# A graph-attention and hypergraph kernel on one core: plain products for the first two pairs' features, another order in the prologue, and the last pair's sums of h on VectorE

## The chip, the cores and the metric

The kernel runs on one core of a Trainium2 chip. A core has TensorE (PE, with its weight loads shown as PEld), VectorE (DVE), ScalarE (ACT), GpSimd (POOL) and SyncE (SP), which here only issues transfers. The metric is the device time of one execution in microseconds (us). The kernel before took 2590.04 us, the median of three runs from 2588.01 to 2591.15.

## The reference

The input x has 128 graphs of 128 nodes with 512 features, adj the 128 x 128 matrix of each graph (0 or 1, with ones on the diagonal). All is float32. Two layers follow one another, each with a residual and a layer norm:

```
feats = x @ W (8 heads of 64)                       # features
dense = leaky(feats.a_self[i] + feats.a_neigh[j]) + BIG * (adj - 1)
att   = softmax(dense, over j);  y = relu(att @ feats + b0)
x1    = layernorm(x + y)

H = (adj != 0);  prop(v) = Dn * H @ (Be * H^T @ v)   # Dn, Be from sums of H and adj's first row
h  = relu(prop(x1 @ W1^T) + b1);  h = layernorm(h) * gamma + beta     # 1024 wide
out = layernorm(x1 + (prop(h @ W2^T) + b2) + x1)
```

## The kernel before, in words

**Tiling.** The graphs are worked off in 64 pairs. Everything of a pair sits in tiles of 128 partitions: its x and adj, the scores nb (2 graphs x 8 heads x 128), the attention's result y, the hidden layer h (1024 wide) and the output o. Weights stay in SBUF throughout. W, W1 and W2 are each cut into a 2 x 2 grid of blocks.

**Three block products.** The features (tile names pf), the hidden layer (ph) and the second product (py) are each computed with seven block products in place of eight. For this the operands need sums and differences of blocks: those of the weights are made once (`prepare_first_sums`, `prepare_hidden`, `prepare_output_block_sums`, all on DVE), those of the data once per pair (`x_sums` on POOL with tile xS, `z_sums` with zS, `h_sums` with hS, through the helper `first_sums`). `chain` puts the seven products in the order 1, 2, 6, 5, 7, 4, 3 as far as its list of times says so: 1, 6, 7 and 4 go on in the same PSUM bank X, from which ACT copies the states after 1, 6 and 7; 2 goes to Y; 5 and 3 to W. `f_sum`, `h_sum` and `y_sum` add the parts up.

**Stages of a pair.** `nodes` computes Dn from adj's first row, turns it with a DVE transpose into the tile dr, and `write_nodes` writes that to DRAM (dd_d), from where `spread_nodes` reads it back to all partitions. `edges` and `scale_edges` make H^T and its scaled copy, `propagator` multiplies the two (pd), `r_evict` gives R. `x_transpose` turns x, the feature product follows, `spread_rows` sends the attention's row terms through DRAM (rd), `neighbours` reads them back to all partitions (nb). POOL adds the mask (`masked`), ACT applies the leaky function and the exponential, DVE finds the maxima in between (`largest`, tile nm). The exponentials are transposed through DRAM (`e_write`, `e_read`, `e_transpose`: tiles ed, eb, eT), for pair 0 alone on PE (`e_transpose_first`, tile pet). `attend` (pav), `attended`, `add_bias` (POOL), `residual`, `rstds`, `first_shift` (sh) and `first_output` (ACT) give x1. `propagate` (pz), the ph chain, `relu`, `square`, `squares` (POOL), `h_sums` (POOL), the py chain, `h_rstd`, `y_scale` and `output` (pq) and the norm end with the store.

**What sets the order.** Each step is entered with a lag in pairs and a time; it is put at (pair + lag) x 38.6 + time. All steps of all pairs and the one-off steps of `todo` are sorted by this number and issued in that order, so each engine's queue is fixed by hand. The function `shift` changes the times of pairs 0 and 1. Each engine works its queue in order. Most work tiles have one buffer, some two (`bufs=2`), so a step also waits until the buffer's former content has been read.

**Transfers.** SP issues nearly all of them, in the same order; a transfer's issue also waits for the landing of the one eight places before it, since eight counters are shared by SP's and ACT's transfers. At the start, code outside the timed list issues them: pair 0's adj, half of w0, pair 0's blocks of x and adj, the other half of w0, pair 1's adj, then w2 (2 MB) and w1 (2 MB). ACT issues seven small loads (attention vectors, biases, gamma, beta).

**Weights' preparation.** `prepare_first` multiplies w0 by the attention vectors (DVE and POOL) and reduces, ACT copies w0 beside the result. `prepare_output` multiplies w2 with gamma and beta on PE (pv, L232), `prepare_output_sums` sends the two rows through DRAM (sums_d, gw, bw_bc), `prepare_output_blocks` scales w2 with them (16 DVE instructions, L254).

Of the kernel before, what the change touches and what calls it, by code (L numbers as in the profile page):

```python
# [20 lines left out]
def kernel(  # L21
# [41 lines left out]

    nc = tc.nc
    G, N, F = x.shape
    P = 128
# [20 lines left out]
        return psum.tile([P, HALF], F32, tag="bank", name=name)  # L89


    st = {}

    def load(p):
        s = st[p] = {}
        gs = slice(2 * p, 2 * p + 2)
        s["a"] = work.tile([P, 2, N], F32, tag="a", name=f"a_{p}", bufs=2)
        nc.sync.dma_start(s["a"], adj[gs].rearrange("g n e -> n g e"))
        s["w"] = work.tile([P, 2, N], F32, tag="w", name=f"w_{p}")
        for g in range(2):  # L100
            nc.sync.dma_start(s["w"][:, g, :], adj[2 * p + g, 0, :].partition_broadcast(P))

    def load_blocks(p):
        s = st[p]
        gs = slice(2 * p, 2 * p + 2)

        s["xb"] = work.tile([P, 2 * NB, P], F32, tag="xb", name=f"xb_{p}")
        rows = x[gs].rearrange("g (b n) (f c) -> f n (g b) c", b=NB, f=NB)
        for f in range(NB):
            nc.sync.dma_start(s["xb"][f * B:(f + 1) * B], rows[f])  # L110

    def load_edges(p):
        s = st[p]

        s["ab"] = work.tile([P, 2 * NB, B], F32, tag="ab", name=f"ab_{p}")
        rows = adj[2 * p:2 * p + 2].rearrange("g (b n) (f e) -> f n (g b) e", b=NB, f=NB)
        for f in range(NB):
            nc.sync.dma_start(s["ab"][f * B:(f + 1) * B], rows[f])

    load(0)  # L120


    def block(dst, ap, i, j, rows, cols):
# [11 lines left out]
    for dst, i, j in ((w0_sb[:, 0], 0, 0), (w0_sb[:, 1], 1, 0), (w0_12, 0, 1), (w0_sb[:, 2], 1, 1)):  # L135
        raw = work.tile([P, KF // 2, QU], F32, tag=("eT", "nb", "sq", "hS")[2 * i + j], name=f"w0_raw{i}{j}")
        nc.sync.dma_start(
            raw, w0.rearrange("(p k) c -> p k c", k=KF)
            [:, i * KF // 2:(i + 1) * KF // 2, j * QU:(j + 1) * QU],
        )  # L140
        if (i, j) == (1, 0):
            load_blocks(0)
            load_edges(0)
        w0_blocks.append((dst, raw.rearrange("p k (h u) -> p k h u", h=HH), j))

    def everywhere(ap, n, name):
# [3 lines left out]

    as_bc = everywhere(a_self, F, "as_bc")
    an_bc = everywhere(a_neigh, F, "an_bc")
    load(1)
    b0_bc = everywhere(b0, F, "b0_bc")
    b2_bc = everywhere(b2, F, "b2_bc")
    bw_bc = const.tile([P, F], F32, name="bw_bc")
# [3 lines left out]
    for t, ap in ((b1_sb, b1), (gb[:, 0, :], gamma), (gb[:, 1, :], beta)):  # L160
        nc.scalar.dma_start(t, ap.rearrange("(k p) -> p k", p=P))

    staged = work.tile([P, 2, DH], F32, tag="h", name="staged")

    w2_sb = const.tile([P, 7, KH // 2, QU + 1], F32, name="w2_sb")
    w2_12 = staged[:, 1, :].rearrange("p (k c) -> p k c", k=KH // 2)
    w2_blocks = ((w2_sb[:, 0, :, :QU], 0, 0), (w2_12, 0, 1), (w2_sb[:, 1, :, :QU], 1, 0),
                 (w2_sb[:, 2, :, :QU], 1, 1))
    for dst, i, j in w2_blocks:
        block(dst, w2t, i, j, DH // 2, QU)  # L170

    w1_sb = const.tile([P, 7, KF // 2, HALF], F32, name="w1_sb")
    w1_21 = staged[:, 0, :].rearrange("p (k c) -> p k c", k=KF // 2)
    for dst, i, j in ((w1_sb[:, 0], 0, 0), (w1_21, 0, 1), (w1_sb[:, 1], 1, 0), (w1_sb[:, 2], 1, 1)):
        block(dst, w1t, i, j, F // 2, HALF)

    ident = const.tile([P, P], F32, name="ident")
    make_identity(nc, ident)
# [8 lines left out]
    dn = const.tile([P, B], F32, name="dn")  # L187
    nc.gpsimd.memset(dn, 0.0)

    def second_sums(eng, w, b12):  # L190

        b11, b21, b22, t4, t1, t2, t3 = (w[i] for i in range(7))
        eng.tensor_tensor(t1, b12, b11, op=ALU.subtract)
        eng.tensor_tensor(t2, b22, t1, op=ALU.subtract)
        eng.tensor_tensor(t3, b22, b12, op=ALU.subtract)
        eng.tensor_tensor(t4, b21, t2, op=ALU.subtract)

    def prepare_first(half):
        for n, (dst, raw, j) in list(enumerate(w0_blocks))[2 * half:2 * half + 2]:
# [8 lines left out]
                nc.vector.tensor_reduce(dst[:, :, :, c], t, AX.X, ALU.add)  # L208

    def prepare_first_sums():  # L210
        second_sums(nc.vector, [w0_sb[:, i] for i in range(7)], w0_12)

    def prepare_hidden(i):
        a11, a12, a22, s1, s2, s3, s4 = (w1_sb[:, i] for i in range(7))
# [31 lines left out]
            nc.sync.dma_start(t, sums_d[c].partition_broadcast(P))  # L246
        made["gw"] = gw

    def prepare_output_blocks():
        gw = made["gw"]  # L250
        for blk, i, j in w2_blocks:
            for k in range(KH // 2):
                c = i * KH // 2 + k
                nc.vector.scalar_tensor_tensor(  # L254
                    blk[:, k, :], blk[:, k, :], gb[:, 0, c:c + 1], gw[:, j * QU:(j + 1) * QU],
                    op0=ALU.mult, op1=ALU.subtract,
                )

    def prepare_output_block_sums():
        second_sums(nc.vector, [w2_sb[:, i, :, :QU] for i in range(7)], w2_12)  # L260
        for i in (0, 1, 5):
            nc.gpsimd.memset(w2_sb[:, i, :, QU:], 1.0 / DH)


    steps = []

    def step(lag, time, skip_first=False):
        def keep(fn):
            steps.append((lag, time, fn, skip_first))
            return fn  # L270
        return keep

    def at(lag, time, fn, *args, skip_first=False):
        step(lag, time, skip_first)(lambda p, s: fn(p, s, *args))

    def chain(kind, lag, times, multiply, w, extra=0):

        tag = "chain" if w == HALF else "half"

        def product(p, s, i):
            where, start = {1: ("X", 1), 2: ("Y", 1), 6: ("X", 0), 5: ("W", 1), 7: ("X", 0),
                            4: ("X", 0), 3: ("W", 0)}[i]
            if start:
                s[kind, where] = bank(f"{kind}{where}_{p}")
            multiply(s, i, s[kind, where], start)

        def copy(p, s, i):
            n = w + (extra if i < 2 else 0)
            t = s[kind, i] = work.tile([P, HALF if w == HALF else FW], F32, tag=f"{tag}_{i}", name=f"{kind}{i}_{p}")
            nc.scalar.copy(t[:, :n], s[kind, "X"][:, :n])  # L294

        for i, t in zip((1, 2, 6, 5, 7, 4, 3), times):
            at(lag, t, product, i)
        for i, t in enumerate(times[7:]):
            at(lag, t, copy, i)

# [103 lines left out]
        first_sums(s, "xS", f"xS_{p}", halves(s["xT"], KF // 2), i, nc.gpsimd, "xS")  # L406

    for i in range(4):
        at(1, 6.1 + 0.7 * i, x_sums, i)

    def rows_product(s, i, a, sums, w, n, nk, extra, to, start):

# [12 lines left out]
    def feature(s, i, to, start):  # L425
# [1 line left out]
                     w0_sb.rearrange("p b k h u -> p b k (h u)"), FW, KF // 2, 0, to, start)  # L427

    chain("pf", 1, (16.2, 17.1, 18.0, 18.9, 19.8, 22.4, 23.3, 17.3, 19.0, 20.8),
          feature, FW)  # L430

    def by_head(t):
        return t[:, :FW].rearrange("p (h u) -> p h u", h=HH)
# [6 lines left out]
        else:  # L440
            nc.vector.tensor_tensor(dst, by_head(s["pf", i]), by_head(s["pf", where]), op=ALU.add)

    at(1, 18.2, f_sum, 0, 0, 0, "Y")
    at(1, 21.4, f_sum, 1, 1, 2, "W")
    at(1, 24.4, f_sum, 0, 1, 1, "W")
    at(1, 23.4, f_sum, 1, 0, None, "X")

    @step(1, 25.0)
    def spread_rows(p, s):
# [110 lines left out]
    for (g, q), tm, (lag, tl), (lagx, tx), te, tt in (  # L560
        ((0, 0), 31.0, (1, 33.2), (1, 33.9), 2.7, 18.1), ((0, 1), 32.2, (1, 35.0), (1, 36.7), 4.6, 18.15),
        ((1, 0), 34.2, (1, 37.5), (2, 2.0), 7.8, 21.5), ((1, 1), 35.4, (2, 6.0), (2, 7.3), 7.9, 21.55),
    ):
        at(1, tm, masked, g, q)
        at(lag, tl, leaky, g, q)
        at(lagx, tx, largest, g, q)
        at(2, te, exponential, g, q)
        at(2, tt, e_transpose, g, q, skip_first=True)

    for g in range(2):  # L570
        at(2, (6.2, 10.9)[g], e_write, g, skip_first=True)
        at(2, (10.0, 14.9)[g], e_read, g, skip_first=True)

# [185 lines left out]

    def h_sums(p, s, i):
        first_sums(s, "hS", f"hS_{p}", halves(s["h"], KH // 2), i,
                   nc.gpsimd, "hS")

    at(3, 20.9, h_sums, 0)
    at(3, 22.2, h_sums, 1)
# [82 lines left out]
    def o_norm(p, s):  # L850
# [4 lines left out]

    T = 38.6
    todo = [
        (11.1, prepare_first, (0,)), (12.0, prepare_first, (1,)), (13.0, prepare_first_sums, ()),
        (65.0, prepare_output, ()), (71.4, prepare_output_sums, ()), (73.7, prepare_hidden, (0,)),
        (75.6, prepare_hidden, (1,)), (77.5, prepare_hidden, (2,)), (77.6, prepare_hidden, (3,)),  # L860
        (82.0, prepare_output_blocks, ()), (83.0, prepare_output_block_sums, ()),
    ]

    def on_pair(fn, p):
        fn(p, st[p])

    def shift(p, lag, time):

        if p == 0:
            if lag == 0:  # L870
                return 2.5 if time < 12.0 else 0.0
            if lag == 1 and 4.0 < time < 10.0:
                return -T + (6.8 if time < 6.0 else 8.0)
            if lag == 2 and time < 8.5:
                return -0.8 * time
        if p == 1 and lag == 1:
            if time < 4.0:
                return -6.0
            return -17.5 if time < 10.0 else -13.0 if time < 12.0 else -23.1 if time < 26.0 else 0.0
        return 0.0  # L880

    for p in range(PAIRS):
        if p > 1:
            todo.append((p * T, load, (p,)))
        if p:
            todo.append((p * T + 19.0, load_blocks, (p,)))
            todo.append((p * T + 28.5, load_edges, (p,)))
        for lag, time, fn, skip in steps:
            if p or not skip:
                todo.append(((p + lag) * T + time + shift(p, lag, time), on_pair, (fn, p)))  # L890
    todo.append((2 * T + 2.1, on_pair, (e_transpose_first, 0)))

    with tc.manual_schedule():
        for _, fn, args in sorted(todo, key=lambda e: e[0]):
# [43 lines left out]
```

## Time and profile before

The profiled execution took 2588.97 us, its span in the trace 2587.2 us, so 1.8 us lie around the span.

| | busy in the span | share |
|---|---|---|
| PE | 2513.1 us | 97% |
| PEld | 2271.3 us | 88% |
| DVE | 2137.3 us | 83% |
| POOL | 1721.5 us | 67% |
| ACT | 1516.3 us | 59% |

In the middle of the run one pair follows the other every 38.6 us. The profile's views used below: the chain of work that ended last, followed back from the last instruction; the list of waits, by waiter and releaser; busy time by stage of the run; and the timeline of one engine, which gives the start of each instruction, its length, the engine, the line of the kernel, what it writes and reads, how many were merged, and in brackets how long the engine had been idle before it and what ended that.

### The profile page before, as it was taken

What the parts mean: (1) busy time and instruction counts of PE and PEld (TensorE: products, weight loads), DVE (VectorE), ACT (ScalarE), POOL (GpSimd) and SP (SyncE); (2) the same over time, 40 slices, a digit from 0 to 9 for tenths busy, and PEclk for the clock granted to TensorE, in tenths of its full rate; (3) what the DMA queues carried; (4) which work ended last, traced back from release to release, by engine and by line L of the source; (5) the groups of instructions that cost most, each with busy time, mean ns of one, the idle gap of its engine ahead of it and who ended that gap; (6) DMA issues with size and microseconds to landing.
All of it is one profiled execution on the core that took longest, in us unless ns stands there. A gap on an engine that the chain in (4) does not pass through costs nothing.

```text
span 2587.2 us, 48238 instructions
## 1 busy us (share of the span) xinstructions
PE 2513.1 (97%) x16304; PEld 2271.3 (88%) x16304; DVE 2137.3 (83%) x4648; ACT 1516.3 (59%) x4297; POOL 1721.5 (67%) x1809
## 2 busy tenths in 40 slices
PE   4799999999999999999999999999999999999997
PEld 2699899899899899899899889999999899999986
DVE  4788888888888888888888888888898888888874
ACT  1465565565565565565565565565565565565562
POOL 3467667667667667667667667667667667766663
PEclk8799999999999999999999999999999999999998
DMA  6344444444444444444444544444444444444430
GB/s 165 106 138 127 149 137 130 141 141 128 143 141 130 145 139 130 146 134 130 144 136 127 150 130 131 144 137 131 142 135 134 142 137 132 143 137 132 143 115 20
DMA packets 428250, 345.57 MB, mean 134 GB/s; under 512 B 146658, under 2 KB 377058, under 8 KB 428004
## 3 DMA queue, kind: packets, MB, share of 16 engines
q1 hardware_dynamic: 424308, 341.43, 43.8%
q8 instruction: 130, 2.13, 0.3%
q10 hardware_dynamic: 3696, 1.06, 0.2%
q14 instruction: 116, 0.95, 0.1%
HBM read 240.66 MB, written 101.72 MB: 132 GB/s over the span
## 4 chain that ended last, share of the span: by engine, by line
PE 91%; DMA 4%; DVE 2%; issue 1%; POOL 1%; ACT 0%; SPq 0%; ACTq 0%; POOLq 0%; DVEq 0%
PE phX L705 18%; PE pyX L418 15%; PE pfX L418 9%; PE phW L705 9%; PE pyW L418 8%; PE pav L579 8%; PE phY L705 4%; PE pz L670 4%; PE pfW L418 4%; PE pq L829 4%; PE pyY L418 4%; PE pfY L418 2%; DMA nb<-rd 2%; PE pd L374 1%; DMA rd<-rows 1%
## 5 line engine op out<-in xcount | busy, mean ns | idle before, releaser
L294 ACT COPY py<-pyX 128x257 f32<-128x257 f32 (+1 forms) x192 | 71.7, 374 | 552.7 <-PE pyX L418 552.7
L705 PEld LDWEIGHTS phX<-zS,w_sb 128*128 128x128 f32 x3072 | 363.0, 192 | 31.2 <-issue 31.2
L499 POOL TENSOR_TENSOR nb<-nb,neg 128x512 f32<-128x512 f32 x256 | 320.3, 1272 | 99.9 <-DMA nb<-rd 54.1
L705 PE MATMUL phX<-zS,w_sb 128*128 128x128 f32 x3072 | 374.2, 275 | 0.7 <-issue 0.7
L756 POOL TENSOR_TENSOR sq<-sq 128x512 f32<-128x512 f32 (+2 forms) x384 | 342.3, 891 | 29.6 <-ACT sq L745 8.6
L506 ACT ACTIVATE nb<-nb,ft 128x128 f32<-128x128 f32 x1024 | 325.4, 390 | 39.1 <-POOL nb L499 34.5
L520 ACT ACTIVATE nb<-nb,nm 128x128 f32<-128x128 f32 x1024 | 320.2, 393 | 1.0 <-DVE nm L512 1.0
L626 POOL TENSOR_TENSOR rso<-veo,mhalf 128x2 f32<-128x2 f32 x64 | 44.8, 700 | 344.9 <-DVE veo L624 329.3
L610 DVE SCALAR_TENSOR_TENSOR y<-y,x 128x512 f32<-128x512 f32 x128 | 154.6, 1208 | 133.2 <-POOL y L603 132.9
L579 PEld LDWEIGHTS pav<-ft,eT 128*128 128x128 f32 x2048 | 252.1, 194 | 11.3 <-DVE eT L541 3.4
L418 PE MATMUL pyX<-w_sb,hS 128*128 128x257 f32 (+1 forms) x1024 | 248.2, 384 | 5.0 <-POOL hS L400 5.0
L579 PE MATMUL pav<-ft,eT 128*128 128x65 f32 x2048 | 246.5, 274 | 3.2 <-DVE eT L541 3.2
L735 ACT ACTIVATE h<-h,b_sb 128x128 f32<-128x128 f32 x768 | 241.2, 392 | 11.6 <-DVE h L720 11.6
L418 PE MATMUL pyW<-w_sb,hS 128*128 128x256 f32 x1024 | 244.1, 380 | 3.5 <-DVE y L788 3.5
L418 PE MATMUL pyX<-w_sb,h 128*128 128x257 f32 (+1 forms) x1024 | 244.3, 381 | 0.0
L418 PEld LDWEIGHTS pyW<-w_sb,hS 128*128 128x128 f32 x1024 | 192.2, 189 | 37.0 <-DVE y L788 9.9
L603 POOL TENSOR_TENSOR y<-y,b_bc 128x512 f32<-128x512 f32 x128 | 162.1, 1266 | 89.4 <-DVE y L594 89.3
L418 PEld LDWEIGHTS pyX<-w_sb,hS 128*128 128x128 f32 x1024 | 190.2, 191 | 30.4 <-POOL hS L400 5.4
L418 PEld LDWEIGHTS pyX<-w_sb,h 128*128 128x128 f32 x1024 | 190.1, 191 | 25.2
L400 POOL TENSOR_TENSOR xS<-xT 128x256 f32<-128x256 f32 x128 | 121.4, 948 | 102.3 <-DVE xT L338 102.3
L512 DVE TENSOR_REDUCE nm<-nb 128x4 f32<-128x512 f32 x256 | 174.2, 680 | 3.8 <-ACT nb L506 1.9
L294 ACT COPY ph<-phX 128x512 f32<-128x512 f32 x192 | 112.4, 585 | 96.4 <-PE phX L705 93.3
(121 smaller groups left out, 5838.5 us busy)
## 6 DMA issues: line engine op xcount, KB each, us to landing
nb<-rd SPq DMA_DIRECT2D x128, 512.0 KB, 5.8
ed<-nb SPq DMA_DIRECT2D x126, 512.0 KB, 3.1
eb<-ed SPq DMA_DIRECT2D x504, 128.0 KB, 2.7
xb<-in_x_dram SPq DMA_DIRECT2D x256, 128.0 KB, 3.0
x<-in_x_dram SPq DMA_DIRECT2D x64, 512.0 KB, 7.1
out_dram<-o SPq DMA_DIRECT2D x64, 512.0 KB, 2.9
a<-in_adj_dram SPq DMA_DIRECT2D x64, 128.0 KB, 6.2
w<-in_adj_dram SPq DMA_DIRECT2D x128, 64.0 KB, 3.8
```

The source lines that it names most:

```text
L294: nc.scalar.copy(t[:, :n], s[kind, "X"][:, :n])
L418: nc.tensor.matmul(to[:, :n], lhs[:, k, :], rhs[:, k, :n], start=bool(start) and k == 0, stop=(k == nk - 1), skip_group_check=True,)
L499: nc.gpsimd.tensor_tensor(t, t, neg[:, :, None, :].to_broadcast([P, NB, HH, B]), op=ALU.add)
L506: nc.scalar.activation(t, t, AF.Prelu, bias=s["ft"][:, g, h, 0:1], alpha=SLOPE)
L512: nc.vector.tensor_reduce(s["nm"][:, g, hs], scores(p, s, g, hs).rearrange("p b h j -> p h b j"), AX.XY, ALU.max, negate=True,)
L520: nc.scalar.activation(t, t, AF.Exp, bias=s["nm"][:, g, h:h + 1])
L579: nc.tensor.matmul(t[:, h * (U + 1):(h + 1) * (U + 1)], s["eT"][:, g, q * HH + h, :], s["ft"][:, g, q * HH + h, 2:], start=True, stop=True,)
L603: nc.gpsimd.tensor_tensor(s["y"][:, g, :], s["y"][:, g, :], b0_bc, op=ALU.add)
L610: nc.vector.scalar_tensor_tensor(y, y, 0.0, s["x"][:, g, :], op0=ALU.max, op1=ALU.add)
L705: nc.tensor.matmul(to[:, m * N:(m + 1) * N], w[:, k, m * P:(m + 1) * P], rhs[:, k, :], start=bool(start) and m == 0 and k == 0, stop=(k == ...
L735: nc.scalar.activation(dst[:, k, :], src[:, k, :], AF.Relu, bias=b1_sb[:, c:c + 1])
L756: nc.gpsimd.tensor_tensor(t[:, :n, :], t[:, :n, :], t[:, n:2 * n, :], op=ALU.add)
```

## The change

It touches three places.

- **First two pairs' features.** Pairs 0 and 1 no longer use the seven-product chain, its sums xS and `f_sum` (`since=2`). `plain_features` does the eight block products directly from w0's four blocks, for each of the two graphs into two PSUM banks; `plain_features_out` moves the banks to the feature tile, two on ACT and two on DVE. w0's block differences are then first used by pair 2, and `prepare_first_sums` is placed later.
- **Prologue.** All of w0 is loaded first, then pair 0's adj; pair 0's blocks of x and adj are issued from ACT. Pair 1's loads, w2 and half of w1 become timed steps behind pair 0's row terms (nb), the other half of w1 comes after pair 1's. `shift` is replaced by a table of times for single steps of pairs 0 and 1. `prepare_output` (pv) now stands between pair 0's two attention products, and w1's and w2's preparation on DVE is placed behind pair 0's first layer, that of w2 in two parts. The tiles that take w1's and w2's odd block are separate ones instead of one.
- **Last pair.** For pair 63 `h_sums` runs on VectorE; its first attention products and what follows on them are placed later, behind the first py product of pair 62; of its own py chain, product 2 is placed ahead of product 6.

The core of the diff:

```diff
-    load(0)
...
-        if (i, j) == (1, 0):
-            load_blocks(0)
-            load_edges(0)
...
-    load(1)
+    load(0)
+    load_blocks(0, nc.scalar)
+    load_edges(0, nc.scalar)
...
-    for dst, i, j in w2_blocks:
-        block(dst, w2t, i, j, DH // 2, QU)
...
+    def load_weights(blocks, ap, rows, cols):
+        for dst, i, j in blocks:
+            block(dst, ap, i, j, rows, cols)
...
+    def plain_features(p, s):
+        s["pf"] = [[bank(f"pf_{p}_{g}{j}") for j in range(2)] for g in range(2)]
+        for i in range(2):
+            for j in range(2):
+                w = (w0_sb[:, 0], w0_12, w0_sb[:, 1], w0_sb[:, 2])[2 * i + j]
+                for g in range(2):
+                    for k in range(KF // 2):
+                        nc.tensor.matmul(
+                            s["pf"][g][j][:, :FW], s["xT"][:, g, i * KF // 2 + k, :],
+                            w[:, k].rearrange("p h u -> p (h u)"), start=(i == 0 and k == 0),
+                            stop=(i == 1 and k == KF // 2 - 1), skip_group_check=True,
+                        )
+
+    def plain_features_out(p, s):
+        s["ft"] = fts[p]
+        for j in range(2):
+            for g in range(2):
+                (nc.scalar.copy, nc.vector.tensor_copy)[g](
+                    s["ft"][:, g, j * HH:(j + 1) * HH, :UW], by_head(s["pf"][g][j])
+                )
...
-                   nc.gpsimd, "hS")
+                   nc.vector if p == PAIRS - 1 else nc.gpsimd, "hS")
...
-        (11.1, prepare_first, (0,)), (12.0, prepare_first, (1,)), (13.0, prepare_first_sums, ()),
-        (65.0, prepare_output, ()), (71.4, prepare_output_sums, ()), (73.7, prepare_hidden, (0,)),
-        (75.6, prepare_hidden, (1,)), (77.5, prepare_hidden, (2,)), (77.6, prepare_hidden, (3,)),
-        (82.0, prepare_output_blocks, ()), (83.0, prepare_output_block_sums, ()),
+        (11.1, prepare_first, (0,)), (12.0, prepare_first, (1,)), (77.9, prepare_first_sums, ()),
+        (11.8, load_blocks, (1,)), (15.65, load, (1,)), (15.7, load_edges, (1,)),
+        (15.8, load_weights, (w2_blocks, w2t, DH // 2, QU)),
+        (16.0, load_weights, (w1_blocks[:2], w1t, F // 2, HALF)),
+        (80.2, load_weights, (w1_blocks[2:], w1t, F // 2, HALF)),
+        (103.0, prepare_output, ()), (116.5, prepare_output_sums, ()),
+        (112.0, prepare_hidden, (0,)), (112.5, prepare_hidden, (1,)),
+        (114.5, prepare_hidden, (2,)), (115.0, prepare_hidden, (3,)),
+        (122.4, prepare_output_blocks, (slice(0, 2),)),
+        (128.4, prepare_output_blocks, (slice(2, 4),)),
+        (130.6, prepare_output_block_sums, (slice(0, 2),)),
+        (132.8, prepare_output_block_sums, (slice(2, 4),)),
+        (100.0, prepare_mean_columns, ()),
...
+    first = {
+        ("nodes", 0): 15.0, ("write_nodes", 0): 16.5, ("spread_nodes", 0): 18.5,
+        ("x_transpose", 0): 11.5, ("edges", 0): 15.2, ("scale_edges", 0): 15.4,
+        ("spread_rows", 0): 13.5, ("neighbours", 0): 14.0, ("load_rows", 0): 14.2,
+        ("propagator", 0): 103.5, ("r_evict", 0): 104.0,
+        ("nodes", 1): 17.6, ("write_nodes", 1): 17.9, ("x_transpose", 1): 14.5,
+        ("edges", 1): 110.4, ("scale_edges", 1): 110.5,
+        ("spread_rows", 1): 79.9, ("neighbours", 1): 80.0,
+        ("propagator", 1): 117.7, ("r_evict", 1): 118.0,
+    }
...
+        (0, plain_features, 12.5), (0, plain_features_out, 13.0), (0, e_transpose_first, 79.3),
+        (1, plain_features, 16.2), (1, plain_features_out, 79.2),
...
+            if p == PAIRS - 1:
...
+                time = {
+                    ("attend", 0): 24.25, ("attended", 0): 25.5, ("add_bias", 0): 25.6,
+                    ("h_sums", 0): 19.1, ("h_sums", 1): 19.2,
+                    ("product", 2): 25.0 if (lag, time) > (3, 20.0) else time,
+                }.get((name,) + args[:1], time)
```

## The prediction

> **What bounds the kernel now.** I read first the chain of work that ended last, then PE's waits in the long middle, then the engines' busy time by stage. The chain's first line:
>
> ```profile
> PE 91%; DMA 4%; DVE 2%; issue 1%; POOL 1%; ACT 0%; SPq 0%; ACTq 0%; POOLq 0%; DVEq 0%
> ```
>
> PE's waits between 134 and 2470 us (waiter, releaser, us in total, times, longest):
>
> ```profile
> PE pyW L418 <- DVE y L788: 3.0, 8, 1.0
> ```
>
> Busy time by stage (stretch, its length, busy us of PE, PEld, DVE, ACT, POOL with counts, then granted clock, DMA share, GB/s):
>
> ```profile
> 0.00:96.40 96.40, 44.67 (x161) 30.17 (x161) 55.86 (x123) 23.64 (x65) 28.42 (x39) 0.77 0.52 139
> 96.40:134.50 38.10, 37.38 (x251) 34.76 (x252) 26.73 (x63) 23.46 (x67) 25.56 (x27) 1.00 0.42 126
> 134.50:2464.40 2329.90, 2326.81 (x15243) 2114.21 (x15242) 1985.21 (x4321) 1415.98 (x4020) 1608.60 (x1680) 1.00 0.46 137
> 2464.40:2541.10 76.70, 73.03 (x478) 66.13 (x478) 54.00 (x112) 42.46 (x119) 44.10 (x46) 0.98 0.27 92
> 2541.10:2587.20 46.10, 31.24 (x178) 25.99 (x177) 15.50 (x33) 10.77 (x28) 14.83 (x17) 0.89 0.06 23
> ```
>
> The middle is PE's alone: it waits 3 us in 2330, and the change leaves the order of every engine there as it was. So only the first 114 us and the last 70 can move. The prologue, from the timelines (start, us, engine, line, what, count, idle before it and its releaser):
>
> ```profile
> 31.88 8.21 SPq L324 DMA_DIRECT2D dd_d<-dr  x2
> 39.51 0.21 DVE L319 STREAM_TRANSPOSE dr<-dn 128x32 f32<-128x32 f32 x1 [4.75 <-DMA dd_d<-dr]
> 43.20 0.23 DVE L453 STREAM_TRANSPOSE rows<-ft 128x32 f32<-128x32 f32 x1
> 51.73 4.92 POOL L499 TENSOR_TENSOR nb<-nb,neg 128x512 f32<-128x512 f32 x4 [1.79 <-DMA nb<-rd]
> 68.31 1.63 DVE L254 SCALAR_TENSOR_TENSOR w_sb<-w_sb,gb,gw 128x256 f32<-128x256 f32 x4
> 92.88 3.38 PE L670 MATMUL pz<-R,y 128*128 128x128 f32 x16 [14.50 <-ACT y L647]
> 114.40 1.90 PE L579 MATMUL pav<-ft,eT 128*128 128x65 f32 x16
> ```
>
> DVE waits 4.75 us for a 16 KB write behind the weights' loads; pair 0's rows leave at 43.4; DVE then prepares w2 from 68.3 to 79.3 before pair 0's attention, so pz waits until 92.88. From pz on PE runs through. The tail:
>
> ```profile
> 2516.23 1.95 PE L705 MATMUL phW<-zT,w_sb 128*128 128x128 f32 x16
> 2521.39 2.63 PE L579 MATMUL pav<-ft,eT 128*128 128x65 f32 x16 [3.21 <-DVE eT L541]
> 2523.82 3.03 PE L418 MATMUL pyX<-w_sb,h 128*128 128x257 f32 x8
> ...
> 2555.15 1.91 PE L418 MATMUL pyX<-w_sb,h 128*128 128x257 f32 x8
> 2562.01 3.80 PE L418 MATMUL pyX<-w_sb,hS 128*128 128x257 f32 x8 [4.96 <-POOL hS L400]
> 2565.60 2.57 PE L418 MATMUL pyY<-w_sb,h 128*128 128x257 f32 x8
> ```
>
> Two gaps, 3.21 and 4.96 us, each followed by matmuls at up to twice their time (3.80 for 1.73 in the middle).
>
> **The Trainium skill.** "TensorE: Matmul & The Clock Gate", Part 1, says PE's clock halves after an idle window of about 3.4 us and comes back after a busy one. The trace agrees on half (264-column matmuls 0.52 us each when cold, 0.222 warm), though pv, started cold, takes about 5.4 us to warm, and pav, 7.09 us on end, doesn't warm it. "SBUF — State Buffer", Who interferes with whom: a DVE instruction with two SBUF inputs and a GpSimd one block each other. Here a 128x528 difference takes 0.67 us alone and 1.04 to 1.22 beside POOL. "DMA: Bandwidth & Descriptors", Queues, rings and completion order: each ring is consumed in order. The write dd_d took 7.5 us behind three loads of w1, and 1.4 with nothing ahead.
>
> **Prologue, step by step.** (1) The w0 loads go first, so DVE and POOL can start at 4.7 rather than 8.3 us. But ACT now issues 15 loads (7 before) ahead of its copies of w0. At 0.45 us each and with the waits for earlier landings (4 to 6 us per load), its last, beta, goes out by about 15 (before, beta's issue alone held ACT 3.3 us). Table load 1.28, copy 0.62: first matmul at 17.0 (bounds 15.3 and 18). DVE's last reduction is done by then.
> (2) Pair 0's plain product has 16 matmuls, 32 passes, against 28, without the sums on POOL and copies between. 5.2 us cold (10 passes), 22 x 0.222: 27.1. Copy 0.42 and transpose 0.23: rows at 27.9, 15.5 us earlier. Pair 1's 32 passes (7.1 warm) follow while PE would wait for exponentials: free, as are POOL's three memsets of 0.17, put where POOL is idle.
> (3) Rows to POOL's mask takes 51.73 - 43.43 = 8.3: mask at 36.2.
> (4) Here the gain sticks. SP issues behind the rows' reads: x, a, w twice, ab four times, w2 four times, w1 twice, and only then pair 0's dd_d. Each waits for a landing some eight loads back. w2 starts at 39 (x landed), its 2 MB and 1 MB of w1 at 360 GB/s (350 to 375 between 21 and 25 us of this trace) take 8.5 from 40.5, and dd_d lands at 49.6. DVE's dr of pair 1 waits for it (one buffer), and behind dr on DVE stand pair 0's maxima, for which ACT's exponentials wait. Without it they would start at 41; they start at 49.9. Bounds 47 and 52.
> (5) Leaky and exponentials, 1.25 per group of four, five left: 56.8. Copies of pair 1's features 0.65, first eT 0.5, two pav cold 3.5, y and gbs 0.9: pv at 62.6. pv now stands between pair 0's two attentions; cold it costs 9.7 (45.94 to 55.67 before), warm 6.9. I take 9.7. The w0 sums fall beside idle POOL and hide. pav, pd, pav 2.2, y 0.6: 75.1. From the last y to pz, 92.88 - 85.79 = 7.1: **pz at 82.1**, 10.7 earlier.
> (6) The preparation that DVE did before pz comes after it. From the shift (sh, done 0.9 ahead of pz, 81.2) to pair 1's first eT, DVE has edges and their scaling 1.8, hidden 4 x 1.13, sums 0.7, 16 scalings of w2 6.3, its four differences 4.7 (18.0 added), and 11.6 as before (maxima 2.4, edges 1.4, transposes 2.1, skip 1.25, scale and nodes 1.7, R 0.3, h 1.8, eT 0.6). 29.6, plus 1 for POOL (0 to 3.5): eT at 111.9. PE is through pf at pz + 21.5 as before + 0.4 for pair 1's pd, at 104.0, and waits 8 us; resuming cold costs 2.4 (5 us at half speed). So pav stands as if begun at 114.3, against 114.4. **Prologue: 0.1 gained, in fact nothing**; bounds -6.6 (load bounds early, pv warm) and +4.8 (late, POOL in the way).
>
> **Tail.** (7) For pair 63, pav of group 0 goes behind py 1 of pair 62: 1.74 us of matmul fills the first gap, PE idles 1.6 and stays warm. py 6 starts at 2524.9 (hS on POOL ends 2524.8) instead of 2528.6. Yet pz then waits for the shifted output, 2536.4 as before, against PE's 2539.1: 2.6 gained, 1.2 if the clock drops anyway.
> (8) Pair 63's sums of h: POOL's three squares 2.7 and three sums 3.8 become DVE sums behind the norm of pair 62's output. On the shifted clock h is ready at 2554.7, DVE free 2555.2, two sums at 0.6 alone or 1.2 beside POOL's squares: 2556.6 to 2557.9. py 2 is pulled ahead of py 6 and fills 1.74. py 6, 7, 5, pm, 4, 3 from 2557.6: five at 1.73 to 1.79, 0.45 for the copy between 6 and 7 that py 2 used to hide, pm 0.15: 2566.9 against 2575.3. The last 11.9 us stay. **Tail: 8.4** (5.5 to 8.9).
>
> Sum: 8.5. The profiled execution took 2588.97 (span 2587.2 and 1.8 around it), 1.07 below the median 2590.04. It becomes 2580.5, the median 2581.
>
> **Rivals.** *Loads in time* (ends lower): dd_d lands when nodes are ready (41) or pv is warm and POOL out of the way. For: 3 MB need only start earlier than SP's waits allow in my count. Against: the 4.75 us wait above. DVE's 29.6 still stands between, so 5 to 9 us: 2572 to 2576. *Prologue eats the tail*: eT is 5 to 9 us later than in (6) because DVE's two-input steps run beside POOL's z and x sums, which take 5.8 us there. For: 0.67 against 1.22. It leaves 2586 to 2590, no change. *The write behind the weights decides* (slower): if dd_d lands after 63.3, 13.7 us past my count, each us comes out at the end and the kernel passes 2595. That needs the 3 MB to move at 3000/22.8 = 130 GB/s; the prologue's mean is 139, which speaks for it, but back-to-back weight loads ran at 350 to 375. Then some 2597 to 2602. That the change does not do what it says is out for the tail: its orders are fixed in the program.
>
> **Numbers.** Main case 0.52, its own range 2577 to 2586; loads in time 0.20; eaten 0.16; slower 0.12. A change of 0.2% (5.2 us) is about what a measurement tells from none. Faster: 0.48 of the main case and 0.20, 0.68. Same: its other 0.04 and 0.16, 0.20. Slower: 0.12. The range 2571 to 2593 leaves out the slow case and a little below.
>
> **What would show it.** Right: first pf matmul near 17; rows near 28; dr waiting for dd_d until about 50; pz near 82; PE idle some 8 us before pair 1's pav near 112; no POOL hS for pair 63, its py 6 within 3 us of py 2; last pyW to end 11.9. Wrong: maxima at 41, no idle before pav, or a cold clock at either tail gap. The prediction fails most easily in (4) and (6), whose waits I count on two queues at once.

## The result and the profile after

In the first comparison the changed kernel took 2587.64 us (median of six runs, 2584.49 to 2589.42) against 2588.60 for the kernel before (six runs, 2585.61 to 2591.15): a ratio of 0.9995, 95% interval 0.9982 to 1.0008. That is no difference that this can measure. A second comparison, beside the experiments below, gave 2584.72 against 2589.93, 0.9980 (0.9971 to 0.9989): 5 us faster (2.8 to 7.5), small, but the interval excludes a ratio of 1. Forecast was 2581, 9 us faster.

The profiled execution of the changed kernel took 2588.48, span 2586.4, against 2588.97 and 2587.2. First the chain of work that ended last, then PE's waits between 134 and 2470 us, as before:

```profile
PE 89%; DMA 4%; DVE 3%; issue 2%; POOL 2%; SPq 0%; ACT 0%; ACTq 0%; POOLq 0%; DVEq 0%
```

```profile
PE pyW L417 <- DVE y L808: 3.2, 6, 1.3
```

PE's share of the chain fell by two points; DVE, POOL and "issue" show one more each (all are rounded). The middle is as it was. Busy time by stage, with the columns of the table before (the last two stretches are cut at this trace's pz of pair 63):

```profile
0.00:96.40 96.40, 51.41 (x229) 38.61 (x230) 46.21 (x109) 27.84 (x78) 25.45 (x35) 0.81 0.53 134
96.40:134.50 38.10, 29.94 (x168) 26.65 (x168) 33.81 (x67) 14.36 (x40) 23.26 (x21) 0.91 0.47 137
...
2464.40:2543.15 78.75, 77.12 (x490) 69.87 (x489) 57.02 (x119) 46.22 (x129) 47.50 (x50) 0.96 0.29 91
2543.15:2586.40 43.25, 31.08 (x195) 26.22 (x193) 21.66 (x40) 11.38 (x29) 10.58 (x13) 0.95 0.07 25
```

In the second stretch PE did 37.4 us of work before and 29.9 now, while DVE went from 26.7 to 33.8. PE gained work ahead of it and lost as much in it: DVE is the busy engine there. The prologue by the timelines (start, us, engine, line, what, count, and the idle time before with its releaser):

```profile
30.29 0.23 DVE L473 STREAM_TRANSPOSE rows<-ft 128x32 f32<-128x32 f32 x1
37.55 4.94 POOL L519 TENSOR_TENSOR nb<-nb,neg 128x512 f32<-128x512 f32 x4 [23.43 <-DMA nb<-rd]
52.67 0.21 DVE L318 STREAM_TRANSPOSE dr<-dn 128x32 f32<-128x32 f32 x1 [9.02 <-DMA dd_d<-dr]
84.71 3.79 PE L690 MATMUL pz<-R,y 128*128 128x128 f32 x16 [7.91 <-ACT y L667]
98.71 3.07 DVE L250 SCALAR_TENSOR_TENSOR w_sb<-w_sb,gb,gw 128x256 f32<-128x256 f32 x4
104.00 1.28 ACT L540 ACTIVATE nb<-nb,nm 128x128 f32<-128x128 f32 x4 [7.03 <-DVE nm L532]
105.84 3.76 PE L725 MATMUL phX<-zS,w_sb 128*128 128x128 f32 x16 [7.10 <-issue]
111.72 2.18 DVE L192 TENSOR_TENSOR w_sb<-w_sb 128x1024 f32<-128x1024 f32 x1
117.71 2.00 PE L599 MATMUL pav<-ft,eT 128*128 128x65 f32 x16 [0.36 <-DVE eT L561]
```

The rows leave 12.9 us earlier than before, pz is 8.2 earlier (84.71 against 92.88), and pav of pair 1 is 3.3 later (117.71 against 114.40). Two waits hold it: dr, with pair 0's maxima behind it, waits 9.02 us for the write; and between pz and pav PE stands still for 7.10. There "issue" names no cause, but the ACT line does: ACT's exponential waited 7.03 us for pair 1's maxima, which stood on DVE behind eight scalings of w2, and ACT's copy of ph, which PE needed, stood behind that exponential. The tail:

```profile
2520.13 1.95 PE L725 MATMUL phW<-zT,w_sb 128*128 128x128 f32 x16
2525.40 5.67 PE L599 MATMUL pav<-ft,eT 128*128 128x65 f32 x32 [1.58 <-DVE eT L561]
2530.86 3.57 PE L417 MATMUL pyX<-w_sb,hS 128*128 128x257 f32 x8
...
2560.95 1.90 PE L417 MATMUL pyY<-w_sb,h 128*128 128x257 f32 x8
2564.62 1.98 PE L417 MATMUL pyX<-w_sb,hS 128*128 128x257 f32 x8 [1.77 <-DVE hS L399]
2572.58 1.89 PE L417 MATMUL pyW<-w_sb,hS 128*128 128x256 f32 x8
```

The first gap shrank from 3.21 to 1.58 us, and still pav and the product behind it ran at a low clock (5.67 and 3.57). The second gap, 4.96 before, is 1.77. Four stretches add up to the span, here with the second profiled execution of the same kernel (the run e7_changed_again below):

| us | before | after | after, again |
|---|---|---|---|
| start to pav of pair 1 | 114.40 | 117.71 | 115.36 |
| to the last phW of pair 62 | 2401.83 | 2402.42 | 2401.62 |
| to pz of pair 63 ("gap A") | 22.86 | 23.02 | 22.85 |
| to the last pyW ("gap B") | 34.34 | 29.43 | 29.43 |
| to the end | 13.77 | 13.82 | 13.74 |
| span | 2587.2 | 2586.4 | 2583.0 |

Only gap B gained, 4.9 us. The prologue gave 3.3 of it back in one execution and 1.0 in the other.

### The profile page after: what moved, and what is told of

The parts are those of the page before. It is cut to its first block, busy times and chain, and to the rows that moved or that the text cites. A ratio compares the mean times of both kernels' runs of the same rounds, so it can differ in the third digit from the quotient of the medians.

```text
span 2586.4 us, 48239 instructions
## 1 busy us (share of the span) xinstructions
PE 2515.8 (97%) x16312; PEld 2274.8 (88%) x16312; DVE 2146.5 (83%) x4650; ACT 1514.4 (59%) x4293; POOL 1714.1 (66%) x1797
## 4 chain that ended last, share of the span: by engine, by line
PE 89%; DMA 4%; DVE 3%; issue 2%; POOL 2%; SPq 0%; ACT 0%; ACTq 0%; POOLq 0%; DVEq 0%
PE phX L725 17%; PE pyX L417 14%; PE phW L725 9%; PE pfX L417 8%; PE pyW L417 8%; PE pav L599 8%; PE phY L725 4%; PE pz L690 4%; PE pq L849 4%; PE pfW L417 4%; PE pyY L417 4%; PE pfY L417 2%; DMA nb<-rd 1%; PE pd L373 1%; DMA dnb<-dd_d 1%
```

## The experiments

All ratios are to the kernel before, run beside each kernel. Its median was 2591.13 beside e1 to e4, 2589.93 beside e5 to e8, 2590.0 beside g1 to g3 and 2590.13 beside the last. The stretches come from each kernel's one trace.

| run | ratio (95% interval) | pz of pair 0 | pav of pair 1 | gap A | gap B |
|---|---|---|---|---|---|
| e1_tail_alone | 0.9967 (0.9956 to 0.9979) | 93.03 | 114.56 | 21.60 | 29.43 |
| e2_prologue_alone | 0.9998 (0.9992 to 1.0005) | 82.33 | 115.21 | 22.87 | 34.41 |
| e3_write_ahead | 0.9945 (0.9933 to 0.9958) | 73.61 | 106.56 | 23.25 | 29.43 |
| e4_maxima_first | 0.9980 (0.9971 to 0.9989) | 82.34 | 114.99 | 21.60 | 29.43 |
| e7_changed_again | 0.9980 (0.9971 to 0.9989) | 82.12 | 115.36 | 22.85 | 29.43 |
| e5_hidden_early | 0.9985 (0.9977 to 0.9992) | 87.23 | 116.69 | 24.50 | 29.43 |
| e6_pool_without_inputs | 0.9972 (0.9961 to 0.9983) | 81.44 | 112.74 | 22.88 | 29.43 |
| e8_together | 0.9947 (0.9935 to 0.9960) | 76.41 | 105.12 | 21.61 | 29.43 |
| g1_dve_order | 0.9960 (0.9947 to 0.9972) | 74.20 | 103.10 | 22.84 | 29.43 |
| g2_all | 0.9943 (0.9929 to 0.9956) | 72.94 | 97.67 | 21.61 | 29.43 |
| g3_all_vectors | 0.9936 (0.9923 to 0.9948) | 69.70 | 94.42 | 21.60 | 29.43 |
| g3_again | 0.9932 (0.9919 to 0.9946) | 69.53 | 94.74 | 22.72 | 29.96 |

### The two halves of the change

The kernel before with the diff's `time = {...}.get(...)` for the last pair and its sums of h on VectorE, and nothing else:

> The kernel before with the last pair's edits alone. Theory (the prologue gives 3 us away, the tail gives back 5): 4 to 6 us faster than before; the stretch from the last phW of pair 62 to pz of pair 63 stays at 22.9 (pav 5.7, the product behind it 3.6, the clock low), that from pz to the last product falls from 34.3 to 29.4. Rival (the prediction's steps 7 and 8): 8.4 us faster, the first of the two stretches 2.6 shorter, its products at 1.8.

And the changed kernel without these:

```
-                   nc.vector if p == PAIRS - 1 else nc.gpsimd, "hS")
+                   nc.gpsimd, "hS")
...
-            if p == PAIRS - 1:
-                time = {...}.get((name,) + args[:1], time)
```

> The changed kernel without the last pair's edits. Theory: 3 to 4.5 us slower than before, pav of pair 1 at about 117.7 against 114.4. Rival (step 6's sum was right and only the profiled execution unlucky): within 1 us of before, pav at 114.4.

The tail alone measured 8.5 us faster (5.4 to 11.4 by the interval), but its trace has only 6.2 of that: 1.26 in gap A, 4.91 in gap B (its span is 4.6 shorter, as its middle ran 1.4 longer). Most of the rest lies in the reference: the traced execution of the kernel before, 2588.97, was 2.2 us quicker than the median beside e1. The prologue alone measured 0.5 faster (2.1 faster to 1.3 slower), with pav 0.8 later in the trace. So theory and rival both missed in part: the prologue costs some 1 us in these traces, and nothing that the times show, not 3, and the 3.3 of the first trace were mostly one late start. In e1 the clock held through the first gap:

```profile
2523.09 3.76 PE L579 MATMUL pav<-ft,eT 128*128 128x65 f32 x32 [1.58 <-DVE eT L541]
2526.68 1.96 PE L418 MATMUL pyX<-w_sb,hS 128*128 128x257 f32 x8
...
2537.59 2.00 PE L418 MATMUL pyW<-w_sb,hS 128*128 128x256 f32 x8 [1.80 <-DVE y L788]
```

pav took 3.76 us and the product 1.96, in place of 5.67 and 3.57, but the last pyW then waited 1.80 us for DVE's sum y, so that only 1.26 reached pz. That sum stands on DVE behind pair 63's scaling, skip and statistics (its first statistics at 2530.82), which POOL's bias step held up behind the sums of h. The gain of a warm clock is thus mostly taken up by this chain.

### The changed kernel again

> The changed kernel itself once more, beside the others. Theory (its profiled execution had its first load of w0 land 2 us late, as no later execution of the same prologue did): first pf matmul at 17.4, pav of pair 1 at 115.2, the prologue 0.8 us slower than before, the tail 4.7 to 6.2 faster; 4 to 5.5 us faster than before in all. Rival (19.4 is its usual start): first pf at 19.4, about 1 us faster than before.

4.2 us less than before in the trace, 5.2 (2.8 to 7.5) by the timed executions. The first matmul started at 18.53 us, between theory and rival; in the eight other kernels that start in the same way it was at 17.3 to 17.7. pz at 82.12 is what the prediction had (82.1), partly by luck: the start was 1.5 us later than forecast, but the clock came up sooner (the second eight pf matmuls took 1.94 us, in the first trace 3.06). The first trace's 84.71 was late from its start. pav came 33.24 us after pz, as in the first trace (33.00).

### The write behind the weights

```
-        ("nodes", 0): 15.0, ("write_nodes", 0): 16.5, ("spread_nodes", 0): 18.5,
+        ("nodes", 0): 15.0, ("write_nodes", 0): 15.75, ("spread_nodes", 0): 18.5,
```

> The changed kernel with pair 0's write of dd_d put ahead of the loads of w2 and w1 on SP. Theory (step 4: the write behind the weights holds dr, the maxima and with them all of pair 0's attention): dr waits for under 1 us, maxima from about 44, pz near 76, pav of pair 1 near 109, 8 to 9 us faster than the changed kernel. Rival (another wait takes its place, the weights or gw landing later, or DVE's list): at most 2 us faster, with DVE or PE waiting for w2 or gw.

```profile
40.59 0.21 DVE L318 STREAM_TRANSPOSE dr<-dn 128x32 f32<-128x32 f32 x1
73.61 3.78 PE L690 MATMUL pz<-R,y 128*128 128x128 f32 x16 [7.90 <-ACT y L667]
94.71 3.75 PE L725 MATMUL phX<-zS,w_sb 128*128 128x128 f32 x16 [6.95 <-issue]
```

dr no longer waits for the write, it runs at 40.59 as soon as pair 1's nodes are ready; pz comes 8.5 us earlier than in the changed kernel's second trace and pav 8.8. One place in SP's queue gave 9 us by the ratios (14 us faster than before against 5). The wait behind it, 6.95 us before phX, was there as before. "DMA: Bandwidth & Descriptors" in the Trainium skill, Queues, rings and completion order, says that each ring is consumed in order. The traces agree: in the changed kernel pair 0's write, issued at 44.04 behind six loads of w2 and w1, landed 8.53 us later; in e3 it was issued at 37.44 ahead of them and landed after 2.1, while pair 1's write of the same size, issued at 41.56 behind the same six, took 8.4.

### What holds PE between pz and pav

```
-        (122.4, prepare_output_blocks, (slice(0, 2),)),
+        (123.2, prepare_output_blocks, (slice(0, 2),)),
```

> The changed kernel with the scalings of half of w2 behind pair 1's last maxima on DVE, not ahead of them. Theory (the sum of DVE's work from the shift to pair 1's first eT sets pav): pav stays at 117.7 within 1, PE's 7 us of idle only move from ahead of phX to ahead of pav. Rival (the copy of ph that stands on ACT behind an exponential waiting for those maxima is the cause): pav 4 to 7 us earlier.

pav at 114.99 against 115.36 in the changed kernel's second trace (the 117.7 of the theory is the late first one), and the ratio the same to the last digit as the changed kernel's: the 7 us of idle broke up into 2.39 before phX, 4.01 before phW (for DVE's sum of h) and 1.54 before pf, and pav itself then ran cold (3.68). The blocked copy on ACT was only where the wait showed; DVE's list decides.

```
-        (112.0, prepare_hidden, (0,)), (112.5, prepare_hidden, (1,)),
-        (114.5, prepare_hidden, (2,)), (115.0, prepare_hidden, (3,)),
+        (103.6, prepare_hidden, (0,)), (103.7, prepare_hidden, (1,)),
+        (103.8, prepare_hidden, (2,)), (103.9, prepare_hidden, (3,)),
```

> The changed kernel with the four sums of w1 on DVE while PE runs pv, where DVE has nothing, not behind pz. Theory (DVE's sum of work from the shift to pair 1's first eT sets pav): that stretch is 4.5 to 5.5 us shorter, pav of pair 1 4 to 5 us earlier, the same off the time. Rival (the wait for pair 1's maxima or gw, or PE's own products, come next at once): at most 1.5 us.

```profile
73.85 1.23 DVE L215 TENSOR_TENSOR w_sb<-w,w_sb 128x1024 f32<-128x1024 f32 x1 [7.62 <-DMA w_sb<-in_w1t_dram]
```

A miss, and neither of the named waits: w1's second half landed only at 73.8, after pv, so the sums held pair 0's R and y behind them. pz came 5.1 us later (87.23), and what DVE's list saved behind pz (29.5 us to pav, not 33.2) was spent ahead of it.

In the next kernel POOL's sums of h, z sums and squares of pair 0 are memsets (these are left out of the computation):

```
+        if name in ("xS_1", "hS_0"):
+            return nc.gpsimd.memset(t[:, i], 0.0)
...
+        if p == 0:
+            return nc.gpsimd.memset(t[:, i], 0.0)
...
+        if p == 0:
+            return nc.gpsimd.memset(t[:, :n, :], 1.0)
```

> The changed kernel in which POOL's z sums, squares and sums of h of pair 0 and its x sums of pair 1 are memsets of the same tiles, which read nothing (these sums are left out, pairs 0 and 1 are not computed). Theory (POOL's two-input steps slow DVE's in this stretch by 3 to 3.5 us): the fourth sum of w1 takes 1.22, the first four scalings 1.63, the differences of w2 1.22 each, and pav of pair 1 comes 3 us earlier. Rival (the steps of DVE are long for what they read, not for POOL): the same durations as before, 1.75, 3.07, 2.18 and 1.47.

Pair 1 has no x sums, as its features are plain products; the x sums that POOL does there are pair 2's, and they stayed. That makes them a control:

```profile
88.06 1.22 DVE L215 TENSOR_TENSOR w_sb<-w_sb 128x1024 f32<-128x1024 f32 x1
94.95 3.08 DVE L250 SCALAR_TENSOR_TENSOR w_sb<-w_sb,gb,gw 128x256 f32<-128x256 f32 x4 [0.18 <-DMA gw<-sums_d]
107.97 1.23 DVE L192 TENSOR_TENSOR w_sb<-w_sb 128x1024 f32<-128x1024 f32 x1
```

The fourth sum of w1 took 1.22 (1.75 beside POOL's z sums), the differences of w2 1.23 and 1.22 (2.18 and 1.47 beside the squares), and the scalings, still beside x sums, 3.08 as ever. From pz to pav it took 31.3 us, not 33.24. At the fourth sum and the first of the two differences POOL stood still; beside the second difference it did memsets. In g1 below the same four scalings run after the x sums and take 1.66. POOL pays as well: a z sum took 1.65 to 1.71 beside DVE's two-input sums and 0.73 without them (e8). "SBUF — State Buffer", Who interferes with whom, says that a DVE instruction with two SBUF inputs contends with a GpSimd one that reads SBUF; the numbers of these steps agree.

### Toward a faster version

e3 with w1's second half loaded ahead of pair 1's rows (80.2 to 77.3), its sums on DVE during pv as in e5, and at the tail pair 62's second product ahead of pair 63's pav:

```
+            if p == PAIRS - 2 and (name,) + args[:1] == ("product", 2) and (lag, time) > (3, 20.0):
+                time = 24.22
```

> The changed kernel with the write of dd_d ahead of the loads of w2 and w1, the second half of w1 loaded ahead of pair 1's rows, its four sums on DVE during pv, and, at the tail, py 2 of pair 62 ahead of pair 63's pav, so that PE has no gap there. Theory (the gains lie on one path and add): pav of pair 1 at 100 to 102, no gap and no cold clock between the last phW of pair 62 and pz of pair 63, which lie 21.6 apart; 19 to 22 us faster than before. Rival (with DVE's list shorter, PE's own list or the transfers of pair 1 set pav): pav at 104 to 106, 14 to 17 us faster.

```profile
57.36 3.57 PE L228 MATMUL pv<-w_sb,gbs 128*2 128x256 f32 x8 [4.16 <-DVE gbs L224]
105.12 3.60 PE L599 MATMUL pav<-ft,eT 128*128 128x65 f32 x16 [0.45 <-DVE eT L561]
```

The rival's outcome, 13.7 us faster, no more than e3. gbs and pair 0's y stood on DVE behind pair 2's nodes, which waited 5.47 us for their adjacency behind the weights, and pz came 2.8 us later than in e3. The sums during pv shortened what follows pz by 4.2 (28.7 against 32.95). At the tail the gap was gone and pav ran warm, as expected, yet the last pyW waited 2.80 us and gap A stayed at 21.61: the sum y on DVE sets it.

Then DVE's order itself, on top of e3:

```
-        (122.4, prepare_output_blocks, (slice(0, 2),)),
+        (128.3, prepare_output_blocks, (slice(0, 2),)),
...
-        (130.6, prepare_output_block_sums, (slice(0, 2),)),
-        (132.8, prepare_output_block_sums, (slice(2, 4),)),
+        (134.0, prepare_output_block_sums, (slice(0, 2),)),
+        (137.5, prepare_output_block_sums, (slice(2, 4),)),
```

> The changed kernel with the write of dd_d ahead of the weights' loads, and on DVE all 16 scalings of w2 behind pair 1's maxima and the second sum of h, and w2's four differences behind pair 1's transposes of the exponentials, two by two. Theory (DVE's list from the shift to pair 1's first eT sets pav, and 5 to 8 us of it are due later): pav at 99 to 101 against 106.6 with the write ahead alone, no wait of PE over 3 us from pz on; 5 to 7 us faster than that kernel, 19 to 21 faster than before. Rival (pair 0's products with w2 now wait for its differences, or PE's own list is next): pav at 104 or later, or the time given back behind it, at most 2 us faster than with the write alone.

```profile
93.40 1.66 DVE L250 SCALAR_TENSOR_TENSOR w_sb<-w_sb,gb,gw 128x256 f32<-128x256 f32 x4
106.05 1.18 DVE L192 TENSOR_TENSOR w_sb<-w_sb,w 128x1024 f32<-128x1024 f32 x1
107.36 3.35 POOL L399 TENSOR_TENSOR hS<-h 128x512 f32<-128x512 f32 x2 [4.21 <-ACT ft L438]
125.86 3.78 PE L417 MATMUL pyW<-w_sb,hS 128*128 128x256 f32 x8 [4.16 <-DVE y L808]
```

pav came at 103.10, 3.5 us earlier than in e3, and the kernel was no faster than e3: the time was given back behind pav. POOL's sums of h lie in the buffer of w_12 (`tag="hS"` for both), whose last reader is the third difference of w2. Put off behind the transposes, it ended at 107.23, and POOL, named as waiting for ACT, started at 107.36; its bias step for pair 1 stood behind the sums. In e6, too, POOL's memsets of hS waited for that difference (4.31 us). PE waited 1.80 us for hS, and 4.16 for y before pair 0's last pyW, where e3 has no wait, and behind the latter the clock was low (3.78). The stretch from pav to the last phW of pair 62 went from 2401.5 to 2410.9. The rival was right, through a buffer that neither had named. To put only the third difference ahead of the transposes was not tried.

The next adds to g1 what e8 had, with pair 2's nodes behind w1's sums (`("nodes", 2): 103.92, ("write_nodes", 2): 103.95`):

> The kernel of g1_dve_order, and with it w1's second half loaded earlier, w1's sums on DVE during pv, pair 2's nodes and their write behind these (in e8_together they held pair 0's y and gbs, and PE 4.16 us), and the filled gap at the tail. Theory: pz near 74, pav of pair 1 at 96 to 98, the tail's first stretch 21.6 without a cold clock; 22 to 24 us faster than before. Rival (PE's own list from pz is what is left, some 24 us): no earlier than g1_dve_order, within 2 us of it.

The last, run twice, has the loads of five vectors on SP in place of ACT as well:

```
-        nc.scalar.dma_start(t, ap.rearrange("(k p) -> p k", p=P))
+            nc.sync.dma_start(t, ap.rearrange("(k p) -> p k", p=P))
...
+        (11.8, load_blocks, (1,)), (11.9, load_vectors, ()),
```

> The kernel of g2_all with the loads of b0, b2, b1, gamma and beta on SP behind pair 1's blocks, not on ACT ahead of its copies of w0. Theory (step 1: ACT's issues hold its table load and copies): table load at 11.5, first pf matmul at 13.5 to 15, DVE's last reduction at 18 next for the second half; 1 to 2.5 us faster than g2_all. Rival (DVE's reductions of w0 set the start anyway): first pf at 16.5 or later, under 1 us.

> The kernel of g3_all_vectors once more, since its profiled execution took 2566.7 and the four timed ones 2573.6 to 2575.4. If the profiled execution was the usual one: first pf matmul near 14, pav of pair 1 near 94.4, 20 us or more faster than before. If the timed ones were: 15 to 17 us faster, and the trace shows where the 7 us go, in the first 120 us (a load that lands late) or in PE's waits for pyW in the middle.

g2 was 14.8 us faster than before (11.4 to 18.4), not the 22 to 24 of its theory, though pav stood at 97.67: from there to the last phW of pair 62 it took 2406.2 us, 4.7 more than in e3, so part of the gain was given back behind pav as in g1. g3's first matmul started at 13.92 in place of 17.3, which shows the ACT queue's part. It has the lowest ratios, 0.9936 and 0.9932, some 17 us (14 to 21) faster than before and, by the ratios, 12 faster than the changed kernel; from g2 its intervals don't separate it. The two profiled executions of g3 differ by 7.3 us in their spans (2565.0 and 2572.3), though pav stands at 94.42 and 94.74. Two lines of the first, then the second:

```profile
94.42 2.90 PE L603 MATMUL pav<-ft,eT 128*128 128x65 f32 x16
117.20 2.00 PE L421 MATMUL pyW<-w_sb,hS 128*128 128x256 f32 x8 [2.85 <-DVE y L812]
```

```profile
94.74 1.90 PE L603 MATMUL pav<-ft,eT 128*128 128x65 f32 x16
117.51 3.78 PE L421 MATMUL pyW<-w_sb,hS 128*128 128x256 f32 x8 [4.17 <-DVE y L812]
121.09 2.98 PE L694 MATMUL pz<-R,y 128*128 128x128 f32 x16
...
2525.59 3.19 PE L421 MATMUL pyW<-w_sb,hS 128*128 128x256 f32 x8 [2.78 <-DVE y L812]
```

In the first, pav ran cold (2.90), PE came later to its waits, the one in front of pyW was 2.85 us, and the clock stayed up (pyW 2.00, pz 1.95). In the second pav was warm, but the wait was 4.17 and the clock dropped (3.78 and 2.98): from pav to the phX behind that pz it took 29.2 us, not 26.5. At the tail a wait of 2.80 cost nothing more in one, and 2.78 in the other was followed by a drop, 1.6 us (1.1 in gap A, 0.5 in gap B). 1.6 us are waits in the middle (2.4 against 4.0). With 0.3 at the start that makes 6.2 of the 7.3; the rest was not traced. The timed executions lay nearer to the second.

## Why the prediction was right and wrong

The time lay in the range of 2571 to 2593. In the main case's own range, 2577 to 2586, it lay in the second comparison alone, and only there can the gain be told from none. The gain was half of the forecast or less: 4.2 us in the second trace, 0.8 in the first, 8.5 forecast. The 4.3 that the second lacks are 1.1 in the prologue, 2.6 in gap A and 0.9 in gap B, less 0.2 elsewhere.

- **Step 1** (first matmul at 17.0) was right in its mechanism: g3 shows that ACT's loads hold the copies. It was 17.3 to 17.7 in most executions and 18.5 and 19.4 in the two of the changed kernel; both lie beyond the bound of 18, and the 19.4 cost 2.4 us in the first trace.
- **Steps 2 and 3**: from the first matmul to the rows 11.1 us, forecast 10.9; from there to the mask 7.0 rather than 8.3.
- **Step 4** was right and, by e3, the costliest point of the change: dd_d landed at 52.6 in the first trace and dr ran at 50.9 in the second, forecast 49.6 to 49.9; the first is beyond the bound of 52, as all before it was late. The loads' rival, that the write comes in time, is out; so is the slower one, as the write landed 11 us before its threshold.
- **Step 5** was right: pv cold, 9.3 us; from dr to pz 32.0, forecast 32.2.
- **Step 6 failed in one term.** DVE's own work was right: 33.85 us from the shift to the first eT, of which 4.1 are excess over the same forms beside an idle POOL (scaling of edges 0.94, fourth sum of w1 0.53, first scalings 1.44, differences of w2 0.96 and 0.25), so 29.7 against 29.6. For 3.2 of it e6 and g1 show that POOL is the cause; for the edges it is the overlap alone (1.42 beside POOL's mask, 0.47 with POOL idle, in one trace). "Plus 1 for POOL (0 to 3.5)" is the term: it is 4.1. The 2.4 us for a cold restart went the other way: PE's idle fell ahead of phX, so the slow products were over before eT and cost nothing. Two errors thus nearly cancel, which is luck: together 1 us too little, and with step 1's late start 3.3 in the first trace.
- **Step 7 failed.** "PE idles 1.6 and stays warm" came true in two of eight executions with this gap of 1.58 us (e1 and e4). In the other six the clock dropped, gap A took 22.8 to 24.5, and nothing was gained, not even the 1.2 that the step allowed for that case. A cold clock at a tail gap is one of the signs of being wrong that the prediction named. Warm it was 1.26, not 2.6: the last pyW waits for y on DVE, which the step had not counted.
- **Step 8** gave 4.9 for 5.8: py 6 started 0.4 later after pz than counted (the two sums on DVE, beside POOL's squares, took 2.6, counted 2.4), and the five products and their copy took 9.85, not 9.3.

So the rival *Prologue eats the tail* had the right outcome in the first comparison with the right cause at half its size (3 us more from POOL, not 5 to 9), helped by the late start; as much was lost at the tail's first gap.

## What to carry to other kernels

When work is moved off one wait, add up the list of the engine that takes it until the next hand-over, and price each two-input step of DVE at what it costs beside POOL (here 1.2 to 1.9 times), since the two will overlap there. A small transfer that a queue of others waits for belongs ahead of bulk loads on its queue: here one place was worth 9 us. Work can be put off only as long as nobody waits for its result or its buffer: g1 moved pav 3.5 us forward and lost more behind it.

## What the runs showed of the hardware that was not expected

- A gap of 1.58 us ahead of pav was enough for the clock to drop in six of eight executions, at differing places (pav 3.76 to 6.21 us for 32 matmuls). "TensorE: Matmul & The Clock Gate", Part 1, gives some 3.4 us of idle, and says that the window runs freely, so that the place depends on where in it the work lies. The spread agrees with the second; 1.58 us does not fit the first unless pav, whose 7.09 us on end do not warm the clock in the kernel before either, counts for little. That was not tried by itself. In the prologue a gap of 1.90 us ahead of the last pfX, whose matmuls have 264 columns, was followed by a cold pav in g2 and the first g3 (2.86 and 2.90) and by a warm one in the second (1.90). Where the tail's gap was filled (e8, g2, both of g3), pav ran warm four times of four.
- So a wait of 2.8 us costs 2.8 us or 4.4, and the same kernel's spans differ by 7 us with the same prologue. Single executions are poor evidence for a few us here; stretches of a trace, compared one by one, told more than the totals.
- DVE and POOL slowed each other: besides DVE's steps, POOL's three squares took 4.4 to 6.1 us beside DVE's scalings and differences, and 2.7 to 2.9 in the tail ahead of pair 63's pz.
